# A decoder layer on one core: dense products whole or in four strips, score fills copied before their maxima

## The chip, the core and the metric

The kernel runs on one core of one Trainium2 chip, in one launch. The metric is the device time of that launch in microseconds, as the median of several runs. The engines are TensorE (PE in the profile, with PEld for its weight loads), VectorE (DVE), ScalarE (ACT), GpSimd (POOL) and SyncE (SP, which here only issues transfers). All data are fp32. One fp32 product appears in the trace as two passes, each a weight load (LDWEIGHTS) and a MATMUL.

## What is computed

There are 16 sequences of 512 tokens with 256 features, and for each a context of 64 rows. Each sequence goes through three blocks, each followed by a layernorm of input plus block:

```python
# 1. gated long convolution and MLP
z  = rmsnorm(u, pre_norm_w) @ in_proj_w.T          # 3 x 256 features
x2, x1, v = split(short_causal_conv3(z) + short_b)
xv = x1 * v
y  = (fftconv(xv, h) + xv * D_skip) * x2           # h: sum of 16 decaying exponentials per feature
y  = y @ out_proj_w.T + u
zm = rmsnorm(y, post_norm_w)
y  = y + (gelu(zm @ l1_w.T) * (zm @ l2_w.T)) @ l3_w.T      # 672 inner features
# 2. causal self attention plus attention to the context, 16 heads of 16
y  = softmax(causal(q k^T / 4)) v  +  softmax(qc kc^T / 4) vc
y  = y @ Wp + bp
# 3. low-rank feed-forward, rank 64, 1024 inner features
H  = gelu((x @ U1) @ V1 + b1);   y = (H @ U2) @ V2 + b2
```

## The kernel before

A front part computes the convolution for all sequences and loads the weights. The main part then works sequence by sequence (a "batch" below). The work is not written in the order in which it runs. Each piece is handed to `Plan.op` with the engines it may run on, an estimated cost, a priority (`prio`, lower is earlier), the buffers it reads and writes, and a function that emits the instructions. `Plan.schedule` plays this through engine by engine with the estimated costs, and `Plan.emit` writes the instructions in that order. So the order on each engine is fixed when the kernel is built, and a changed cost or rule can move work anywhere in it. Buffers come from small fixed sets: in PSUM one `scores` tile of four banks, one `av` bank and three `mm` banks; in SBUF among others three `ex` tiles of 128x2048.

TensorE can be used as one array of 128x128, or be divided: into four row groups of 32 (products of 32 rows, one per head), into column groups of 32 or 64, or both. The shape (rows, columns) of a part is the `tiling` of an op; `FULL` is 128x128. A stretch below is a run of matmuls with one tiling. `Plan.change` shifts priorities so that ops of one tiling gather: an op that would leave the whole array waits (`HOLD`, 1000), an op of the tiling in force goes first (`STAY`, 1000). Score fills are `urgent` and are held back by neither. `EMPTY` is the cost that the planner adds at a change of tiling.

The steps in the text, by their lines in the profile:

- Dense products on the whole array: the MLP's first two products L1187 and its third L1239, the output projection L1148, the value projection L1268, the query and key projections L1340 (`project`), the attention's output L1083 (`to_tokens`), the feed-forward's first and last L1761 and L1807, and the context's keys and values L1292 and L1317. The MLP's remaining 32 inner features are L1217, 128x32.
- Transposes L348, L1507 (of the maxima) and L1359, on the whole array; also L518 in the front.
- Score fills. Each takes the one `scores` tile, [128, 4 heads, 512]. Per batch there are 12 for the row maxima (L1435, 32x128; three per group of four heads, of 320+192, 448+64 and 512 columns), 10 for the exponentials (L1557, 32x128), and 2 against the context (L1615, 32x64).
- Maxima (`maxima`, `mx_op`): VectorE adds the causal mask to the diagonal blocks in PSUM (L1484) and takes maxima there (L1486, L1489, L1492, L1494, L1495, L1497). In the batches of `COPIED`, that is 0, 1, 13, 14 and 15, ScalarE instead copies the fill to an `ex` tile (L1458), GpSimd masks the copy with affine selects (L1465), and VectorE takes the maxima of the copy.
- Exponentials: ScalarE L1527 from the `scores` tile to an `ex` tile, GpSimd zeroes the upper triangle (L1574), and TensorE makes the weighted sums into `av` (L1587, 128x32; L1635 for the context, 64x32).
- Feed-forward: L1778 (64x128), gelu L1786 on ScalarE, L1794 (128x64).

In batches 0, 1 and 15 the fills are made and used in two halves. The MLP's and feed-forward's gelus and the attention's exponentials are kept in phases: a batch's gelus come between the exponentials of the batch before and its own. The feed-forward of batches 0 to 10 is planned beside the attention of batches 2 to 12, that of 11 and 12 beside batch 15, and that of 13 to 15 at the end; batches 13 and 14 have none beside them.

```python
COPIED = (0, 1, B - 3, B - 2, B - 1)
```

Of the kernel before, what the change touches and what calls it, by code (L numbers as in the profile page):

```python
# [24 lines left out]
FULL = (P, P)  # L25
SLOT_OF = (1, 0, 2, 3)
# [25 lines left out]
class Op:  # L52


    def __init__(self, n, engines, cost, lat, prio, fn):
        self.n, self.engines, self.cost, self.lat, self.prio, self.fn = n, engines, cost, lat, prio, fn
        self.deps, self.users, self.bufs = set(), [], []
        self.ready, self.start, self.end, self.engine = 0.0, None, None, None
        self.tiling, self.urgent = FULL, False


class Plan:
# [9 lines left out]
    def __init__(self, tiles, hold=0, stay=0):  # L72
        self.tiles, self.ops = tiles, []
        self.HOLD, self.STAY = hold, stay

    EMPTY = {P: 0.215, P // 2: 0.16, P // 4: 0.145}

    def op(self, engines, cost, fn, prio, r=(), w=(), lat=0.0, after=(), tiling=FULL, urgent=False, holds=()):
        o = Op(len(self.ops), engines.split(), cost, lat, prio, fn)
        o.tiling, o.urgent = tiling, urgent  # L80
# [14 lines left out]
    def change(self, o, tiling):  # L95

        if o.tiling == tiling:
            return -self.STAY if tiling != FULL else 0
        if o.urgent or o.tiling == FULL:
            return 0  # L100
        return self.HOLD if tiling == FULL else -self.STAY / 2

    def schedule(self):
# [29 lines left out]
        while left:  # L133
# [4 lines left out]
            for e in self.ENGINES:  # L138
# [24 lines left out]
                if e == "PE" and o.tiling != tiling:  # L163
                    o.empty = self.EMPTY[tiling[1]]
                    tiling = o.tiling
                else:
                    o.empty = 0.0
# [22 lines left out]
    def emit(self):  # L190
        for o in self.schedule():
            for b in o.bufs:
                b.t = self.tiles[b.cls][b.slot[1]]
            o.fn(o.engine)
# [3 lines left out]
def decoder_layer(  # L198
# [96 lines left out]
    ROWS4, ROWS2, COLS4, COLS2, BOTH = (SLOT, P), (P // 2, P), (P, SLOT), (P, P // 2), (P // 2, SLOT)  # L295
# [76 lines left out]
    with ExitStack() as front:  # L372
# [283 lines left out]
        for blk in range(NR // R8):  # L656
# [43 lines left out]
            plan.op("PE", 1.0, near_mm, pc - 60, r=[XV[kh], NEAR], w=[ps], tiling=COLS4, holds=[st])  # L700
# [61 lines left out]
            far_done = plan.op("PE", 1.0, far_mm, pc + 10, r=[st, far], w=ys, tiling=(SLOT, P // 2))  # L762
# [270 lines left out]
    plan = Plan(pool, 1000, 1000)  # L1033
# [40 lines left out]
    def to_tokens(xT, w, res, prio):  # L1074

        for cp in range(NT // 2):
            ps = Buf("mm")
            for cc in range(2):

                for k in range(KD):  # L1080

                    def mm(e, cp=cp, cc=cc, k=k, ps=ps):
                        nc.tensor.matmul(  # L1083
# [4 lines left out]
                    plan.op("PE", pe(D), mm, prio, r=[xT], w=[ps])  # L1088
# [18 lines left out]
    def first_block(b, after):  # L1107
# [33 lines left out]
        for cp in range(NT // 2):  # L1141
            ps = Buf("mm")
            for cc in range(2):

                for k in range(KD):

                    def outp(e, cp=cp, cc=cc, k=k, ps=ps):
                        nc.tensor.matmul(  # L1148
# [4 lines left out]
                    plan.op("PE", pe(D), outp, p0, r=[(yt, k)], w=[ps], after=after)  # L1153
# [26 lines left out]
        for f in range(NF):  # L1180
            halves = []
            for w in (w_l1, w_l2):
                ps = Buf("mm")
                for k in range(KD):

                    def mm(e, f=f, w=w, k=k, ps=ps):
                        nc.tensor.matmul(  # L1187
# [3 lines left out]
                    gelus_pe[b].append(plan.op("PE", pe(T), mm, p1 - k, r=[(zT, k)], w=[ps]))  # L1191
# [21 lines left out]
        def mm_e(e, ps=ps):  # L1213
            for n, w in enumerate((w_l1, w_l2)):
                for k in range(KD):
                    for c in range(NT):
                        nc.tensor.matmul(  # L1217
# [4 lines left out]
        gelus_pe[b].append(plan.op("PE", 0.88, mm_e, p1, r=[zT], w=[ps], tiling=COLS4))  # L1222
# [10 lines left out]
        for cp in range(NT // 2):  # L1233
            ps = Buf("mm")
            for cc in range(2):
                for f in range(NF + 1):

                    def mm(e, c=2 * cp + cc, cc=cc, f=f, ps=ps):
                        nc.tensor.matmul(  # L1239
# [6 lines left out]
                    plan.op("PE", pe(D), mm, p2, r=[(gT, f) if f < NF else gE], w=[ps])  # L1246
# [4 lines left out]
    def attention(b, x_):  # L1251
# [9 lines left out]
        for jp in range(NT // 2):  # L1261
            ps = Buf("mm")
            for jj in range(2):

                for k in range(KD):

                    def mm(e, jp=jp, jj=jj, k=k, ps=ps):
                        nc.tensor.matmul(  # L1268
# [4 lines left out]
                    plan.op("PE", pe(D), mm, p0 + 40, r=[(xT, k)], w=[ps])  # L1273
# [12 lines left out]
        if b % 2 == 0:  # L1286
# [3 lines left out]
            def kc_mm(e, ps=ps):  # L1290
                for g in range(G):
                    nc.tensor.matmul(  # L1292
# [4 lines left out]
            plan.op("PE", 0.9, kc_mm, p0, w=[ps], after=begun)  # L1297
# [19 lines left out]
            lambda e, ps=ps: nc.tensor.matmul(  # L1317
                ps.t[:, 0:D], twice.t.rearrange("c s t -> c (s t)"), wcv_s, start=True, stop=True
            ),
            p0 + 45, r=[twice], w=[ps],  # L1320
# [13 lines left out]
        def project(dst, w, cols, bias, prio):  # L1334
            ps = Buf("mm")

            for k in range(KD):

                def mm(e, k=k):
                    nc.tensor.matmul(ps.t, w[:, k, cols], xT.t[:, k, :], start=(k == 0), stop=(k == KD - 1))  # L1340

                plan.op("PE", pe(T), mm, prio - k, r=[(xT, k)], w=[ps], holds=[dst])
# [63 lines left out]
        def maxima(g):  # L1406
# [8 lines left out]
            for use in (((1, TC), (0, TC)), ((2, TC), (3, None)), ((3, 0),)):  # L1415
# [10 lines left out]
                for h, cols in enumerate(cuts):  # L1426

                    def mm(e, use=use, sc=sc, cols=cols):
                        at = 0
                        for i, first in use:  # L1430
                            k0, k1 = (0, TC) if first is None else (TC - first, TC + (i + 1) * P)
                            lo, hi = max(at, cols.start), min(at + k1 - k0, cols.stop)
                            for r in range(HPG if lo < hi else 0):
                                hd = bass.ts(r, SLOT)
                                nc.tensor.matmul(  # L1435
# [6 lines left out]
                        "PE", cost_pe / len(cuts), mm, ps_, r=[q, kk], w=[(sc, h)], tiling=ROWS4, urgent=True  # L1442
# [8 lines left out]
                if b in COPIED:  # L1451
# [18 lines left out]
                    n = HPG * P * (2 if use[0][0] == 1 else 1)  # L1470
                    plan.op("POOL", 0.65 * n / (HPG * P), masked, ps_ - 6, w=[both])
                    sc, cost = both, cost - dve(n)

                def mx_op(e, sc=sc, i=use[0][0], diagonal=diagonal):
                    own = mx.t[:, :, :, HD + par : HD + par + 1]
                    ctx_ = mx.t[:, :, :, par : par + 1].rearrange("p i r o -> p r i o")
                    by_64 = sc.t.rearrange("p r (a c) -> p r a c", c=TC)
                    if b not in COPIED:
                        diag, mask = diagonal(sc.t), mask_qk.unsqueeze(1)
                        if i == 1:  # L1480
                            mask = mask.unsqueeze(1).to_broadcast([P, HPG, 2, P])
                        else:
                            mask = mask.to_broadcast([P, HPG, P])
                        nc.vector.tensor_tensor(diag, diag, mask, ALU.add)  # L1484
                    if i == 1:
                        nc.vector.tensor_reduce(  # L1486
                            ctx_[:, :, SLOT_OF[1] : SLOT_OF[1] + 2, :], by_64[:, :, 0:6:5, :], AX.X, ALU.max, negate=True
                        )
                        nc.vector.tensor_reduce(  # L1489
# [441 lines left out]
```

## Time and profile before

| | |
|---|---|
| runs | 2082.22, 2083.39, 2087.12 us; median 2083.39 |
| span of the profiled execution | 2082.0 us, first to last instruction; the median run is 1.4 us above it |
| granted TensorE clock | 0.992 of full over the span |
| TensorE | 2005.5 us busy (96%), 14,900 passes and as many weight loads |
| VectorE, ScalarE, GpSimd | 1331.5 (64%), 1029.1 (49%), 768.5 us (37%) |
| instruction queue q8 | 117 packets, 1.92 MB (16 KB each) |
| transfers | 88 GB/s on average; 27.6% of the 16 engines' span |

Busy time of an engine is the union of its instructions' times; matmuls that run abreast are counted once. The ends of matmuls are modelled, so a PE that is called busy need not be streaming; the text reads distances from start to start. The trace gives no time of the profiled execution besides its span; the lowest run is 0.2 us above that span.

Group rows read: line, engine, operation, output<-inputs, shape of the weights (rows*columns of the array), shapes, count | busy us, mean ns of one. The mean of matmuls that run four abreast is the time of one of them, while busy us / count is its share.

### The profile page before, as it was taken

The numbers are of one execution on the slowest core, as the hardware profiler recorded it, in microseconds if no ns is written. First come the engines' busy times: TensorE is split into PE (matmuls) and PEld (weight loads), VectorE is DVE, ScalarE is ACT, GpSimd is POOL, SyncE is SP. The second block draws the span as 40 slices with busy tenths as digits, with TensorE's granted clock in tenths as the row PEclk, the third lists the DMA queues.
The fourth block names the chain that finished last, engine by engine and source line by source line (L and its number), as shares of the span: only waits on it lengthen the run. The fifth ranks groups of instructions, "written<-read, shape, count | busy, mean of one in ns | idle before, by whom it ended". The sixth has DMA issues, their size and how long they took to land. (4 is left out here: it accounts for less than half of the span.)

```text
span 2082.0 us, 36834 instructions
## 1 busy us (share of the span) xinstructions
PE 2005.5 (96%) x14900; PEld 1054.2 (51%) x14900; DVE 1331.5 (64%) x1922; ACT 1029.1 (49%) x1463; POOL 768.5 (37%) x1036
## 2 busy tenths in 40 slices
PE   8999978999999999999999999999999999999987
PEld 4455645555554545454545454454545454545443
DVE  7987543736584848484857576666767584656554
ACT  7863422656435262717161626253534446655773
POOL 7694622243323241414142424232323233533432
PEclk9999989999999999999999999999999999999999
DMA  5365861040304040313131312222131404031200
GB/s 200 109 211 179 269 221 51 6 119 17 119 11 144 12 134 22 123 33 118 37 108 48 100 56 88 68 71 85 58 98 33 123 13 129 17 101 44 72 22 31
DMA packets 114939, 182.22 MB, mean 88 GB/s; under 512 B 13393, under 2 KB 62034, under 8 KB 114642
## 3 DMA queue, kind: packets, MB, share of 16 engines
q1 hardware_dynamic: 113234, 177.26, 27.6%
q8 instruction: 117, 1.92, 0.4%
q10 hardware_dynamic: 1536, 2.62, 0.4%
q14 instruction: 52, 0.43, 0.1%
HBM read 111.09 MB, written 68.76 MB: 86 GB/s over the span
## 5 line engine op out<-in xcount | busy, mean ns | idle before, releaser
L1527 ACT ACTIVATE ex<-scores 128x2048 f32<-128x2048 f32 (+1 forms) x228 | 362.5, 1606 | 193.4 <-PE scores L1557 140.8
L1187 PE MATMUL mm<-xT,w_l 128*128 128x512 f32 x640 | 299.5, 608 | 0.0
L1574 POOL TENSOR_SCALAR_AFFINE_SELECT ex<-ex 128x512 f32<-128x512 f32 x256 | 159.1, 637 | 324.5 <-ACT ex L1527 323.1
L1435 PE MATMUL scores<-keys,q 32*128 32x192 f32 (+5 forms) x2848 | 225.3, 426 | 6.2 <-ACT ex L1458 4.6
L1557 PE MATMUL scores<-q,keys 32*128 32x256 f32 (+3 forms) x2240 | 183.3, 435 | 11.8 <-ACT ex L1527 10.9
L1435 PEld LDWEIGHTS scores<-keys,q 32*128 32x128 f32 x2848 | 123.8, 184 | 138.5 <-issue 41.1
L1786 ACT ACTIVATE row<-mm,b_s 128x512 f32<-128x512 f32 x124 | 79.0, 687 | 224.6 <-PE mm L1778 223.9
L1187 PEld LDWEIGHTS mm<-xT,w_l 128*128 128x128 f32 x640 | 114.5, 190 | 141.4 <-issue 133.9
L1717 POOL TENSOR_TENSOR nd<-nd,nd 128x1024 f32<-128x1024 f32 x30 | 70.8, 2358 | 299.2 <-DMA nd<-di 299.2
L1587 PE MATMUL av<-ex,va 128*32 128x512 f32 (+3 forms) x2048 | 164.8, 438 | 0.9 <-POOL ex L1574 0.9
L1239 PE MATMUL mm<-w_l,gT 128*128 128x256 f32 x640 | 160.6, 386 | 0.0
L308 POOL TENSOR_SCALAR small<-small 128x4 f32<-128x4 f32 (+1 forms) x66 | 13.3, 201 | 393.7 <-DVE small L1047 358.8
L500 DVE SCALAR_TENSOR_TENSOR frow<-fmm,cw,frow 128x511 f32<-128x511 f32 x192 | 141.1, 744 | 25.9 <-ACT frow L492 21.2
L1484 DVE TENSOR_TENSOR scores<-scores,mask_qk 128x1024 f32<-128x1024 f32 x132 | 115.6, 876 | 60.9 <-PE scores L1435 57.8
L1557 PEld LDWEIGHTS scores<-q,keys 32*128 32x128 f32 x2240 | 96.9, 184 | 107.5 <-ACT ex L1527 67.0
L1199 ACT ACTIVATE row<-mm 128x512 f32<-128x512 f32 x80 | 47.8, 598 | 209.4 <-PE mm L1187 209.4
L1458 ACT COPY ex<-scores 128x1024 f32<-128x1024 f32 (+1 forms) x96 | 114.4, 1228 | 65.6 <-PE scores L1435 52.9
L485 PE MATMUL fmm<-fx,inw 128*128 128x512 f32 x312 | 143.4, 604 | 0.0
L1239 PEld LDWEIGHTS mm<-w_l,gT 128*128 128x128 f32 x640 | 117.2, 190 | 44.6 <-issue 31.1
L299 DVE COPY row<-av 128x512 f32<-128x512 f32 x60 | 41.5, 692 | 134.9 <-PE av L1587 124.5
L1340 PE MATMUL mm<-xT,wqc_s 128*128 128x512 f32 x256 | 126.3, 611 | 0.0
L1346 DVE TENSOR_SCALAR q<-mm,bqc_s 128x512 f32<-128x512 f32 x62 | 46.5, 750 | 100.4 <-PE mm L1340 100.3
(212 smaller groups left out, 3489.3 us busy)
## 6 DMA issues: line engine op xcount, KB each, us to landing
dn<-row SPq DMA_DIRECT2D x120, 256.0 KB
keys<-dk SPq DMA_DIRECT2D x64, 256.0 KB
nd<-dn SPq DMA_DIRECT2D x30, 512.0 KB
nd<-di SPq DMA_DIRECT2D x30, 512.0 KB
fx<-hpad SPq DMA_DIRECT2D x28, 512.0 KB
early<-gates SPq DMA_DIRECT2D x16, 512.0 KB
early<-yconv SPq DMA_DIRECT2D x32, 256.0 KB
dk<-row SPq DMA_DIRECT2D x32, 256.0 KB
```

What stands on the lines that cost most here:

```text
L485: nc.tensor.matmul(ps.t, inw[:, k, bass.ts(m, P)], xT.t[:, k, :], start=(k == 0), stop=(k == KD - 1))
L500: lambda e, lag=lag: nc.vector.scalar_tensor_tensor(t.t[:, lag:], ps.t[:, 0 : T - lag], cw[:, m, 2 - lag : 3 - lag], t.t[:, lag:], ALU.mul ...
L1187: nc.tensor.matmul(ps.t, w[:, k, bass.ts(f, P)], zT.t[:, k, :], start=(k == 0), stop=(k == KD - 1))
L1239: nc.tensor.matmul(ps.t[:, bass.ts(cc, D)], gT.t[:, f, bass.ts(c, P)] if f < NF else gE.t, w_l3[:, f, :] if f < NF else w_l3e[:, c, :], st ...
L1340: nc.tensor.matmul(ps.t, w[:, k, cols], xT.t[:, k, :], start=(k == 0), stop=(k == KD - 1))
L1435: nc.tensor.matmul(sc.t[:, r, lo:hi], q.t[hd, bass.ts(i, P)], kk.t[hd, k0 - at + lo : k0 - at + hi], start=True, stop=True,)
L1458: lambda e, sc=sc, both=both, cols=cols: nc.scalar.copy(both.t[:, :, cols], sc.t[:, :, cols]),
L1484: nc.vector.tensor_tensor(diag, diag, mask, ALU.add)
L1527: lambda e: nc.scalar.activation(ex.t.rearrange("p (r n) -> p r n", r=HPG)[:, :, cols], sc.t[:, :, cols], AF.Exp, scale=scale),
L1557: nc.tensor.matmul(sc.t[:, r, lo:hi], keys[g].t[hd, TC + j * P : TC + (j + 1) * P], qas[g].t[hd, q0 + lo : q0 + hi], start=True, stop=True,)
L1574: lambda e, ex=ex, at=at: nc.gpsimd.affine_select(out=ex.t.rearrange("p (r n) -> p r n", r=HPG)[:, :, at : at + P], in_=ex.t.rearrange("p ...
L1587: nc.tensor.matmul(av[g].t[bass.ts(r, SLOT), j * P :], va.t[:, j, h * VS : h * VS + SLOT], ex.t[:, r * T + at : r * T + at + n], start=(j ...
```

## The change

Three things change.

First, dense ops are marked `flex`. In the main part such an op is emitted by `Plan.matmul`, either as one product on the whole array or as four products of 32 columns each (`STRIPS`, 128x32). `Plan.mode` picks the form: as it stands if the array is whole or in strips, and strips from any other tiling. The whole array and strips both count as plain in `Plan.change`. Transposes stay whole.

Second, other tilings are brought to few: all scores use `ROWS` = 32x64 (so a fill's 32x128 product becomes two), the feed-forward's second product and the context's sums use `BOTH` = 64x32, and the feed-forward's third product uses strips. The planner's cost of a change becomes a formula of the old and the new tiling.

Third, `COPIED` takes in all batches, and `mx_op` becomes one op per reduction. The mask add of VectorE (L1484) is gone.

The same three changes in the diff, cut to its core:

```diff
+STRIPS = (P, SLOT)
...
-    EMPTY = {P: 0.215, P // 2: 0.16, P // 4: 0.145}
+    ENTRY = {P: 0.104, P // 2: 0.051, P // 4: 0.024}
+
+    def empty(self, old, new):
+
+        return 0.0 if old == new else 0.087 + 0.0066 * P * P / (old[0] * old[1]) + self.ENTRY[new[1]]
...
     def change(self, o, tiling):
 
-        if o.tiling == tiling:
-            return -self.STAY if tiling != FULL else 0
+        want, plain = self.mode(o, tiling), (FULL, STRIPS) if self.strips else (FULL,)
+        if want == tiling:
+            return -self.STAY if tiling not in plain else 0
         if o.urgent or o.tiling == FULL:
             return 0
-        return self.HOLD if tiling == FULL else -self.STAY / 2
+        return self.HOLD if tiling in plain else -self.STAY / 2
+
+    def mode(self, o, tiling):
+
+        return (tiling if tiling in (FULL, STRIPS) else STRIPS) if o.flex else o.tiling
+
+    def matmul(self, out, weights, moving, **kw):
+
+        rows, cols = self.now
+        n = weights.shape[-1]
+        for c in range(0, n, cols):
+            cs = slice(c, min(c + cols, n))
+            self.nc.tensor.matmul(out[cs], weights[:, cs], moving, **kw)
...
-    ROWS4, ROWS2, COLS4, COLS2, BOTH = (SLOT, P), (P // 2, P), (P, SLOT), (P, P // 2), (P // 2, SLOT)
+    COLS2, ROWS, BOTH = (P, P // 2), (SLOT, P // 2), (P // 2, SLOT)
...
-                        nc.tensor.matmul(
+                        plan.matmul(
                             ps.t, w[:, k, bass.ts(f, P)], zT.t[:, k, :], start=(k == 0), stop=(k == KD - 1)
                         )
 
-                    gelus_pe[b].append(plan.op("PE", pe(T), mm, p1 - k, r=[(zT, k)], w=[ps]))
+                    gelus_pe[b].append(plan.op("PE", pe(T), mm, p1 - k, r=[(zT, k)], w=[ps], flex=True))
...
-                        "PE", cost_pe / len(cuts), mm, ps_, r=[q, kk], w=[(sc, h)], tiling=ROWS4, urgent=True
+                        "PE", cost_pe / len(cuts), mm, ps_, r=[q, kk], w=[(sc, h)], tiling=ROWS, urgent=True
...
-                plan.op("DVE", cost, mx_op, ps_ - 5, r=[sc], w=[(mx, par)])
+                for n, (size, views) in enumerate(reduces):
+
+                    def reduce(e, views=views):
+                        dst, src = views()
+                        nc.vector.tensor_reduce(dst, src, AX.X, ALU.max, negate=True)
+
+                    plan.op("DVE", dve(HPG * size), reduce, ps_ - 5, r=[sc], w=[(mx, (par, use[0][0], n))])
...
             def hm(e, fp=fp, bank=bank):
-                for s in range(2):
-                    half = bass.ts(s, RANK)
-                    nc.tensor.matmul(bank(s), v1_s[half, bass.ts(fp, P)], pT.t[half, :], start=True, stop=True)
+                for c in range(0, P, SLOT):
+                    for s in range(2):
+                        half, at = bass.ts(s, RANK), fp * P + c
+                        plan.matmul(bank(s)[c : c + SLOT], v1_s[half, at : at + SLOT], pT.t[half, :], start=True, stop=True)
...
-    COPIED = (0, 1, B - 3, B - 2, B - 1)
+    COPIED = range(B)
```

The other dense products get `plan.matmul` and `flex=True` in the same way, the other fills `ROWS`, and L1794's op `STRIPS`.

## The prediction

> **What bounds it now.** I read the page first, then busy time by batch, then who waits for whom, then the order of TensorE's work. The page names TensorE, and its slices show that this holds almost everywhere:
>
> ```profile
> PE 2005.5 (96%) x14900; PEld 1054.2 (51%) x14900; DVE 1331.5 (64%) x1922; ACT 1029.1 (49%) x1463; POOL 768.5 (37%) x1036
> PE   8999978999999999999999999999999999999987
> ```
>
> A batch begins where its first L1435 fill starts: 452.8 us for batch 1, 990.3 for 6, 1098.4 for 7, 1749.4 for 13, 1941.8 for 15; batches 2 to 12 take 108 to 109 us each. Busy time by such stretches (stretch, length, PE, PEld, DVE, ACT, POOL):
>
> ```profile
> 990.30:1098.40 108.10, 107.77 (x751) 54.45 (x750) 71.35 (x101) 47.91 (x62) 33.67 (x44) 1.00 0.24 75
> 1749.40:1847.10 97.70, 96.70 (x715) 50.78 (x714) 59.79 (x83) 60.67 (x57) 42.77 (x58) 1.00 0.19 57
> 1847.10:1941.80 94.70, 92.76 (x655) 45.08 (x654) 58.05 (x80) 55.59 (x42) 32.20 (x49) 1.00 0.22 68
> ```
>
> TensorE idles 0.33 us in batch 6. Batches 13 and 14 already copy and mask as the change does everywhere; there it idles 1.0 and 1.9. ScalarE's waits in batch 6 point at TensorE, not the other way:
>
> ```profile
> ACT row L1786 <- PE mm L1778: 18.3, 3, 14.7
> ACT row L1199 <- PE mm L1187: 17.3, 5, 4.2
> ACT ex L1527 <- PE scores L1557: 9.5, 8, 2.0
> ```
>
> But a busy TensorE is not one that streams. In its order of time (start, length, line, shape of the weights, count of passes; one fp32 product is two passes):
>
> ```profile
> 1001.89 3.70 PE L1187 MATMUL mm<-xT,w_l 128*128 128x512 f32 x8
> 1005.52 1.15 PE L1435 MATMUL scores<-keys,q 32*128 32x320 f32 x16
> 1006.60 4.56 PE L1187 MATMUL mm<-xT,w_l 128*128 128x512 f32 x10
> 1011.09 1.20 PE L1435 MATMUL scores<-keys,q 32*128 32x448 f32 x16
> 1012.22 2.84 PE L1187 MATMUL mm<-xT,w_l 128*128 128x512 f32 x6
> ...
> 1057.70 1.06 PE L1587 MATMUL av<-ex,va 128*32 128x512 f32 x8
> 1058.69 1.56 PE L1148 MATMUL mm<-outw,early 128*128 128x256 f32 x6
> ...
> 1071.16 1.11 PE L1615 MATMUL scores<-q,kcs 32*64 32x512 f32 x16
> 1072.20 1.13 PE L1340 MATMUL mm<-xT,wqc_s 128*128 128x512 f32 x2
> ...
> 1077.05 1.09 PE L1635 MATMUL mm<-ex,vc 64*32 64x512 f32 x16
> 1078.07 0.66 PE L348 MATMUL mm<-ident,y 128*128 128x128 f32 x4
> ```
>
> From start to start, 8 whole passes take 3.63 us and 10 take 4.49: 0.43 each (0.427 within a stretch), so a stretch costs 3.63 - 8 x 0.427 = 0.2 us besides its passes. The tiled stretches in view hold two rounds of 512 columns, 0.853 us, so L1587 (four abreast, 128x32) costs 0.99 - 0.853 = 0.14 extra, L1615 (eight, 32x64) 1.04 - 0.853 = 0.19, L1635 (eight, 64x32) 0.165. Medians over the trace: whole 0.198, 32x128 0.217, 64x128 0.204, 128x64 0.151, 128x32 0.137, 32x64 0.191, 64x32 0.164. These are the change of tiling and the first load of weights, exposed. The kernel has 1,083 stretches.
>
> **Part 1: tilings.** From 452.8 to 1941.8 us (batches 1 to 14) the trace holds 885 stretches: 328 whole, 309 of 32x128, 35 of 64x128, 44 of 128x64, 113 of 128x32, 28 each of 32x64 and 64x32. Times the prices: 64.9 + 67.1 + 7.1 + 6.6 + 15.5 + 5.3 + 4.6 = 171 us. I relabel the same order by the diff: L1435, L1557 and L1615 become 32x64; L1778 and L1635 64x32; L1794, L1587 and L1217 128x32; a flexible dense product takes 128x32, unless a transpose (L348, L1507) has just made the array whole. That leaves 806: 78 whole, 328 of 128x32, 337 of 32x64, 63 of 64x32, so 15.4 + 44.9 + 64.4 + 10.3 = 135 us. Saved: 36 us, on the path throughout, as TensorE idles 0.3 us a batch there. Outside, relabelling saves 2.3 us before and 2.7 after; those stretches have idle time (the tail is 118.34 busy of 140.20), so I count 2. The planner may put an order with fewer whole stretches in place of the old one: 0 to 10 us more, not counted.
>
> The passes themselves should cost the same. Strips of 128x32 run four abreast: 512 L1587 passes of 512 columns take 68.2 us busy, 133 ns each, 0.53 per four with their share of the changes; L1615 at eight abreast 29.0 us for 416, 0.56 per eight; a whole L1187 pass 299.5 / 640 = 0.47. A 24-pass L1587 stretch comes out 16 ns over its price, so the bound for strips is 0 to 1 ns a pass. No row has four strips reading the same moving columns; I take the same rate, because L1587's four already read four different ones.
>
> A page speaks against this: the Trainium skill, "TensorEngine Tiling (Array Packing)", section Instruction Overhead, gives each matmul about 60 cycles of overhead. Taken one after another at the 2.4 GHz of the skill's "TensorE: Matmul & The Clock Gate" (its opening table), 13,174 more passes would be an estimated 329 us, and the sum 2375 us. The trace disagrees: sixteen L1615 passes cost 0.19 us beyond streaming, all told.
>
> The 448+64 fills (L1435 at 1011.09) take 1.13 us against 1.07 for L1557's eight-pass fill: a weight load of 128 columns outlasts 64 columns of moving data. With 64-column loads most of that 0.06 goes; about 60 fills, 3 us.
>
> **Instructions.** Relabelled, 2,354 dense passes become four, 5,088 score passes two, L1778's and L1794's passes four and two: 14,900 grows to 28,074, each with its weight load. The instruction queue's 117 packets of 16 KB become about 219. After 480 us the mean rate rises from 14 to 29 instructions a us. Nothing waited for a packet there; in the front, at 60 a us, L745 waited up to 2.3 us for "issue" around a fetch. Bound 0 to 20 us; I take 1, since 256 instructions still last some 8 us.
>
> **Part 2: copies.** Batches 2 to 12 have 132 maxima fills. VectorE loses its mask adds: 61.4 + 54.2 = 115.6 us (L1484). ScalarE gains 132 copies of 1.867 us (L1458) = 246, to 1,275 or 62% of the new span; per batch 47.9 + 22.4 = 70 of some 105. GpSimd gains 176 selects of 0.637 (L1465) = 112. Both have idle time, and the reductions take the same from copies (2.28 against 2.29 us). The one scores tile is freed after 1.87 us instead of 1.23 + 0.69 + 1.22 + 0.68 = 3.8, 3.1 or 3.0: three fills hold it 5.6 us, not 9.9. Batch 6's twelve maxima fills, 990.3 to 1052.4 us, need at least 12 x 1.07 + 4 x 9.9 + 12 x 0.35 for the hand-overs = 56.6 of their 62.1; with copies about 39. So the chain fills-to-maxima, close behind TensorE, moves away, and TensorE is late next. New waits: the next fill waits for ScalarE, behind whose copy gelus and evacuations queue; the reductions wait for GpSimd, and behind its masks queue the gate and divide products (2.36 us each at most). A copying batch idled TensorE 0.7 to 1.6 us more than batch 6: 8 to 18 us over eleven, though batches 13 and 14 have no feed-forward products to fill in; at best the present 0.33 goes, -4. I take +4, nearer the low end because these batches keep that filler.
>
> **Sum.** 2082.0 - 36 - 2 - 3 + 1 + 4 = 2046; the median run stands 1.4 us over the span: **2047 us**, 1.7% less. What a measurement here can tell from no change is 0.3%, 6 us.
>
> **Rivals.**
> - *Better order* (0.07): besides, the planner drops whole stretches (10) and the waits inside the paired L1778 stretches shrink (9 of 3.01 us, where passes and price make 1.91: about 10 us in all). 2047 - 20 = 2027, and 2019 with the copies at -4.
> - *ScalarE holds the scores tile* (0.13): its copies come late behind gelus and exponentials, as 70 us of 105 in order leave less slack. Price: the 18 us bound and up to twice it in place of 4, 2061 to 2079. For: "scores <- ACT" waits already exist. Against: ScalarE at 62% in batch 13 cost TensorE 1 us. It cancels the gain at 0.3 us per copied fill.
> - *Instruction supply* (0.12, mostly the slower side): strips double the instructions, fetches come 2 to 3 us late in the middle already (359 instructions between two, where a packet holds 256), and a packet missed costs 2.3 us as at L745. Slower by 6 us needs 42 / 2.3 = 18 stalls among some 180 fetches after 450 us, one in ten; one in five gives 2130. Against: before, none in the middle, and the front ran 600 instructions in 10 us without one.
> - *Forecast* (0.68): 2030 to 2061, by the copies at -4 to 18 and half of the better order.
>
> **Numbers.** Faster: 0.68 + 0.07 + 0.10 of ScalarE's 0.13 = 0.85; the same: 0.03 + 0.02 of supply's = 0.05; slower: 0.10. The range 2029 to 2078 leaves out about 0.05 below and 0.14 above.
>
> **What would show it.** Right: some 28,000 PE passes, about 990 stretches, 128x32 the commonest shape on L1187, L1239 and L1340; batches 2 to 12 at 105 to 106 us; L1484's group gone, L1458 with 132 more; PE still at 99% there. ScalarE rival: "PE scores <- ACT ex" of tens of us. Supply rival: PE waits on "issue" of 1 to 3 us beside instruction packets. The forecast is wrong if a stretch of dense strips takes longer from start to start than 0.427 us a pass, by even 15 ns: 2,354 x 15 ns = 35 us.

## The result and the profile after

The kernel after takes 2112.56 us (median of 4 runs, 2109.03 to 2119.49) against 2083.86 us for the kernel before on the same chip: a ratio of 1.014 [1.0118, 1.0163]. It is slower by 1.4%; the prediction was 2047 us, with a range of 2029 to 2078. The profiled execution took 2110.6 us, its span is 2108.9 us, 26.9 us longer than before.

Two lines of the page of the kernel after, busy time and the slices:

```profile
PE 1978.7 (94%) x27210; PEld 887.1 (42%) x27210; DVE 1237.1 (59%) x1828; ACT 1248.9 (59%) x1557; POOL 877.9 (42%) x1212
PE   8999888899987999999999999999999999989787
```

The passes nearly doubled, and TensorE is busy 26.8 us less than before. But it now idles 2108.9 - 1978.7 = 130.2 us, against 76.5 before. The idle time isn't spread: the slices show 8 in places that had 9, and 7 near the end. By stretches of the kernel after (stretch, length, PE, PEld, DVE, ACT, POOL, then the granted clock, the DMA share and GB/s):

```profile
553.10:635.00 81.90, 76.20 (x923) 34.94 (x923) 54.15 (x75) 40.47 (x50) 28.05 (x35) 1.00 0.18 56
635.00:785.60 150.60, 138.57 (x2073) 55.73 (x2072) 74.09 (x114) 95.93 (x91) 56.21 (x85) 0.99 0.27 83
1001.50:1107.20 105.70, 104.40 (x1477) 42.46 (x1473) 63.94 (x93) 65.48 (x67) 43.03 (x60) 1.00 0.25 72
1953.00:2106.00 153.00, 124.02 (x2016) 50.69 (x2012) 81.14 (x154) 89.90 (x120) 46.76 (x74) 0.95 0.10 31
```

A middle batch (1001.5) is as forecast, 105.7 us, though its neighbours take 110.2. Batches 2 and 3 (the first two rows) and the tail (the last, which ends 2.9 us before the span does) hold 17.7 and 29 us of idle time. Batch by batch, from first maxima fill to first maxima fill, in the profiled executions; two experiments stand beside them:

| us | before | after | e1: old order | e12: one constant |
|---|---|---|---|---|
| up to batch 2 | 554.9 | 553.1 | 555.8 | 554.2 |
| batches 2 and 3 | 218.5 | 232.5 | 212.6 | 217.0 |
| batches 4 to 12 | 976.0 | 969.7 | 951.3 | 960.3 |
| batch 13 | 97.7 | 96.9 | 95.1 | 96.6 |
| batch 14 | 94.7 | 100.8 | 91.8 | 92.8 |
| batch 15 and tail | 140.2 | 155.9 | 139.8 | 138.2 |
| span | 2082.0 | 2108.9 | 2046.4 | 2059.1 |

So three places lose 14.0, 6.1 and 15.7 us, and the middle gains 6.3 where it should have gained some 25 (e1 gains 24.7). In that middle TensorE idles 20.1 us of 969.7, against 3.9 of 951.4 in e1; so most of the difference is waiting.

What a stretch costs is as predicted. TensorE in its order of time, kernel after (L122 is the line of `plan.matmul`, which now records all products but transposes):

```profile
1003.56 1.92 PE L122 MATMUL mm<-xT,w_l 128*32 128x512 f32 x16
1005.42 1.12 PE L122 MATMUL scores<-keys,q 32*64 32x448 f32 x32
1006.47 2.78 PE L122 MATMUL mm<-xT,w_l 128*32 128x512 f32 x24
1009.18 1.11 PE L122 MATMUL scores<-keys,q 32*64 32x512 f32 x16
```

A 448+64 fill takes 1006.47 - 1005.42 = 1.05 us (1.13 before), and 24 strips 2.71 (six rounds of 0.427 and 0.14 for the change: 2.70). The trace holds 976 stretches where about 990 were forecast.

What is new is what TensorE waits for (the waits of PE over the span, kernel after: engine, line, releaser, us in total, times, longest):

```profile
PE scores L122 <- ACT ex L1480: 26.6, 31, 2.1
PE scores L122 <- ACT ex L1553: 24.2, 30, 2.1
```

That is 50.8 us of fills that wait for ScalarE's copies (L1480) and exponentials (L1553); before, the like rows added up to 15.5. ScalarE itself in the batch at 1001.5 still waits for TensorE (its waits in that batch):

```profile
ACT ex L1480 <- PE scores L122: 12.1, 11, 1.9
ACT ex L1553 <- PE scores L122: 7.7, 8, 2.0
```

Both waits are true at once: the fill waits for the one `scores` tile to be read, and ScalarE for the fill. A chain of fill, read, fill runs at its own pace of over 3 us, and TensorE is only idle in it where it has nothing else to do. Why it has nothing else is to be seen in its order around 615 us, kernel after (`row,v_s` is the feed-forward's second product, `scores<-q,keys` a fill for exponentials):

```profile
613.94 1.09 PE L122 MATMUL mm<-row,v_s 64*32 64x512 f32 x16
614.96 1.06 PE L122 MATMUL av<-row,u_s 128*32 128x512 f32 x8
...
618.72 3.64 PE L122 MATMUL mm<-outw,early 128*32 128x256 f32 x64
...
635.00 1.12 PE L122 MATMUL scores<-keys,q 32*64 32x320 f32 x32
636.05 1.09 PE L122 MATMUL mm<-row,v_s 64*32 64x512 f32 x16
638.14 1.12 PE L122 MATMUL scores<-q,keys 32*64 32x512 f32 x16 [1.01 <-ACT ex L1480]
...
642.50 2.01 PE L122 MATMUL scores<-q,keys 32*64 32x384 f32 x32 [2.14 <-ACT ex L1553]
```

The last of the four second products comes at 636.05, 22 us after the third. The exponentials' fills depend on all four (the phases: a batch's gelus before its exponentials), so the first of them is at 638.14. From 616.98 to 635.00 TensorE works off the next batch's projections and output products in plain tilings, with no fill among them; then the exponentials run without those products, and up to 785.6 their fills wait 10.9 us for ScalarE's exponentials. The same stretch in e12, the kernel after with one constant of the planner changed:

```profile
612.54 1.09 PE L122 MATMUL mm<-row,v_s 64*32 64x512 f32 x16
613.56 1.07 PE L122 MATMUL av<-row,u_s 128*32 128x512 f32 x8
614.56 1.09 PE L122 MATMUL mm<-row,v_s 64*32 64x512 f32 x16
...
616.58 1.11 PE L122 MATMUL scores<-q,keys 32*64 32x512 f32 x16
...
626.66 1.48 PE L122 MATMUL mm<-outw,early 128*32 128x256 f32 x24
```

Here the fourth product is in place at 614.56, the exponentials begin at 616.58, and the projections and output products lie between their fills.

The code says how a product can be held. `hm` (L1778 before) is not urgent, so in a plain tiling `Plan.change` puts it back by 1000, the distance in priority between two batches, and it goes only when nothing that then ranks before it is ready, the next batch's dense products among it. Before, the third product that precedes it (128x64) was no plain tiling, and from there `change` drew it forward by 500. Now the third product, the weighted sums and the dense products are all in strips, and strips count as plain.

### The profile page after: what moved, and what is told of

The parts are those of the page before. It is cut to its first block, busy times and chain, and to the rows that moved or that the text cites. A ratio compares the mean times of both kernels' runs of the same rounds, so it can differ in the third digit from the quotient of the medians.

```text
span 2108.9 us, 61825 instructions
## 1 busy us (share of the span) xinstructions
PE 1978.7 (94%) x27210; PEld 887.1 (42%) x27210; DVE 1237.1 (59%) x1828; ACT 1248.9 (59%) x1557; POOL 877.9 (42%) x1212
## 4 chain that ended last, share of the span: by engine, by line
PE 59%; ACT 8%; DVE 4%; issue 2%; DMA 2%; POOL 1%; SPq 0%; POOLq 0%; ACTq 0%; DVEq 0%
PE mm L122 36%; PE scores L122 15%; PE av L122 7%; ACT ex L1553 3%; DVE maxes L1523 2%; ACT ex L1480 2%; PE mm L370 1%; ACT row L1813 1%; DVE q L1542 1%; ACT xt L1089 1%; PE mm L1533 1%; ACT L1553 1%; DMA nd<-di 1%; DMA di<-sums 1%; POOL nd L1743 1%
## 5 line engine op out<-in xcount | busy, mean ns | idle before, releaser
L1523 DVE TENSOR_REDUCE maxes<-ex 128x8 f32<-128x512 f32 (+4 forms) x384 | 448.3, 1210 | 69.4 <-POOL ex L1487 60.0
L1480 ACT COPY ex<-scores 128x2048 f32<-128x2048 f32 (+1 forms) x228 | 360.6, 1598 | 209.5 <-PE scores L122 181.2
L1553 ACT ACTIVATE ex<-scores 128x2048 f32<-128x2048 f32 (+1 forms) x228 | 362.4, 1606 | 163.5 <-PE scores L122 148.6
L122 PE MATMUL mm<-xT,w_l 128*32 128x512 f32 (+2 forms) x2880 | 318.2, 541 | 4.1 <-DVE gT L1226 4.0
L1487 POOL TENSOR_SCALAR_AFFINE_SELECT ex<-ex 128x512 f32<-128x512 f32 x256 | 159.5, 638 | 385.5 <-ACT ex L1480 385.4
L1600 POOL TENSOR_SCALAR_AFFINE_SELECT ex<-ex 128x512 f32<-128x512 f32 x256 | 159.3, 637 | 305.9 <-ACT ex L1553 305.2
L122 PE MATMUL scores<-keys,q 32*64 32x192 f32 (+5 forms) x5696 | 219.9, 410 | 23.7 <-ACT ex L1480 23.6
L122 PE MATMUL scores<-q,keys 32*64 32x256 f32 (+3 forms) x4480 | 181.7, 423 | 25.3 <-ACT ex L1553 20.9
L122 PEld LDWEIGHTS scores<-keys,q 32*64 32x64 f32 x5696 | 103.4, 132 | 176.2 <-ACT ex L1480 100.2
L122 PE MATMUL av<-ex,va 128*32 128x512 f32 (+3 forms) x2048 | 167.4, 438 | 2.4 <-POOL ex L1600 2.3
L122 PE MATMUL mm<-w_l,gT 128*32 128x256 f32 (+1 forms) x1900 | 164.2, 387 | 2.4 <-DVE q L1542 2.4
L122 PEld LDWEIGHTS mm<-xT,w_l 128*32 128x32 f32 (+1 forms) x2880 | 88.2, 111 | 175.3 <-issue 154.4
L122 PEld LDWEIGHTS scores<-q,keys 32*64 32x64 f32 x4480 | 80.2, 131 | 141.8 <-ACT ex L1553 79.0
L122 PE MATMUL mm<-xT,wqc_s 128*32 128x512 f32 (+1 forms) x802 | 123.8, 594 | 0.0
L122 PEld LDWEIGHTS mm<-w_l,gT 128*32 128x32 f32 (+1 forms) x1900 | 91.4, 120 | 71.7 <-issue 38.7
```

The source lines that it names most:

```text
L122: self.nc.tensor.matmul(out[cs], weights[:, cs], moving, **kw)
L1480: lambda e, sc=sc, both=both, cols=cols: nc.scalar.copy(both.t[:, :, cols], sc.t[:, :, cols]),
L1487: nc.gpsimd.affine_select(out=part, in_=part, compare_op=ALU.is_ge, fill=NEG, base=0, pattern=[[0, HPG], [-1, P]], channel_multiplier=1,)
L1523: nc.vector.tensor_reduce(dst, src, AX.X, ALU.max, negate=True)
L1553: lambda e: nc.scalar.activation(ex.t.rearrange("p (r n) -> p r n", r=HPG)[:, :, cols], sc.t[:, :, cols], AF.Exp, scale=scale),
L1600: lambda e, ex=ex, at=at: nc.gpsimd.affine_select(out=ex.t.rearrange("p (r n) -> p r n", r=HPG)[:, :, at : at + P], in_=ex.t.rearrange("p ...
```

## The experiments

Times are medians of 3 rounds, ratios against the kernel before on the same chip. The runs stand on several chips, on which the kernel before takes 2082.6 to 2084.4 us; so a difference between two runs of different chips is good to some 2 us.

**The order or the prices.** e1 emits all new tilings, but plans the order with the old tilings, the old `EMPTY` table and the old rule; copies in the five batches and maxima in one op, as before:

```diff
-    tiling=ROWS, urgent=True
+    tiling=ROWS4, made=ROWS, urgent=True      # planned as, emitted as; so for every op
-    COPIED = range(B)
+    COPIED = (0, 1, B - 3, B - 2, B - 1)
```

> The order on every engine is that of the kernel before (planned with its tilings, its costs and its rule), and maxima are taken as before; only the tilings that are emitted are those of the change. The trace of after shows the price of each stretch as predicted. Theory A (the loss comes with the order that the planner makes): about 2083.9 - 36 - 2 - 3 = 2043 us, 1.9% under before, about 990 stretches. Rival C (the strips themselves do harm, by their instructions or on the engines around them): no gain, 2080 to 2115.

2044.72 us, 0.9813 [0.9799, 0.9828], the fastest kernel of this study. This is the prediction's sum without its copies, 2082 - 36 - 2 - 3 + 1 + 1.4 = 2043. From batch 1 to batch 14 the trace of e1 holds the 806 stretches of the relabelling, shape by shape (78, 328, 337 and 63), and these batches take 1451.9 us against 1489.0. A middle batch (980.10 on, kernel e1; PE busy 104.86 of 105.30):

```profile
980.10:1085.40 105.30, 104.86 (x1553) 42.53 (x1549) 71.01 (x101) 48.01 (x62) 33.61 (x44) 1.00 0.25 76
```

e2 is the change with its own rule and formula, only `COPIED` and `mx_op` as before:

> The tilings, the planner's costs and its rule of the change; copies in batches 0, 1, 13, 14 and 15 alone, as before. If the loss of after (some 70 us of waits, against 45 saved on stretches) comes with the copies: about 2045 us. If it comes with the order under the new rule: 2090 to 2115.

2194.44 us, 1.0532 [1.0516, 1.0548], outside both expected ranges. Without the copies the loss is nearly four times as large, so it doesn't need the copies. In its middle batches a second product is left behind each time: one is at 1085.73, the last at 1108.31, and between them lie 17 us of plain products.

e3 adds the copies alone to the kernel before (`COPIED = range(B)`), e4 also splits `mx_op` into one op per reduction:

> The kernel before with copies in all batches, the maxima of a fill still one op. If the loss comes with the copies: 2083.9 + 50 to 70 = 2135 to 2155 us, with TensorE waiting for ScalarE ahead of fills. If it comes with the new rule: within 10 us of before.

> As the run with copies alone, but with one op for each reduction, as in the change. If the size of the op matters (a shorter op lets other VectorE work in between): 5 us or more under that run; otherwise the same as it within 5 us.

2092.89 us, 1.0046 [1.0028, 1.0063], and 2097.15 us, 1.0065 [1.0049, 1.0082]. Copies cost a little at the old tilings (8.5 us). Splitting the maxima adds 4.3 us by the medians, which isn't clear of the noise: the intervals overlap, and from batch 2 on the two profiles have the same times batch by batch to 0.1 us.

**The second product.** e5 is the kernel after, e6 is e2, each with one word:

```diff
-    plan.op("PE", tiled(T), hm, p3, r=[pT], w=hp, tiling=BOTH)
+    plan.op("PE", tiled(T), hm, p3, r=[pT], w=hp, tiling=BOTH, urgent=True)
```

> The changed kernel, with one word more: the feed-forward's second product (64x32, line L1778 of the kernel before) is marked urgent, so the planner no longer adds 1000 to its rank while the array is whole or in strips. Theory H: this product is held until a fill opens another tiling; the exponentials' fills may only come after its gelus; so both stand still while the next batch's dense products run, and the exponentials later lack filler. Then most of the 68 us between after and the old order come back: 2050 to 2070 us. Rival (the copies, or the rest of the new rule): 2095 us or more.

> The tilings with the new rule, copies in five batches alone, and the feed-forward's second product urgent. Theory H: from 2194 to 2050 to 2080 us, with TensorE's waits for ScalarE ahead of exponentials' fills down from 122 us to under 40. Rival (another part of the new rule): over 2150 us.

e6: 2066.33 us, 0.9931 [0.991, 0.9952], 128 us less than e2. The wait of e2 that goes (PE waits of e2, then of e6, by the same line):

```profile
PE scores L122 <- ACT ex L1549: 122.2, 123, 2.4
```

```profile
PE scores L122 <- ACT ex L1549: 19.8, 24, 1.7
```

So e2's loss was the held product. The other profiles agree: only in the kernel after, e2, e13 and e18 does batch 2's fourth second product come 20 us or more after the third (in all others within 6 us). Batches 2 and 3 of the kernel after, e13 and e18 take 231.2 to 232.9 us, and e2, where a product is held in every middle batch, takes 1065.9 for batches 4 to 12; the others take 211.8 to 222.0 and 949.6 to 987.5. e5 took 2094.71 us, 1.0059 [1.0039, 1.008]: 18 us less than the kernel after, but where the rival put it and not at 2050 to 2070. The loss in batches 2 and 3 is gone (217.8 against 232.5), but batches 4 to 12 now take 985.1 against 969.7.

**The steps one by one.** e7 is e1 with the copies everywhere; e8 is e7 planned with the formula, in place of the table, for the tilings as emitted:

> All three parts of the change are emitted, but the order is planned with the tilings, costs and rule of the kernel before (copies in all batches, one op per fill). Copies alone cost 2092.9 - 2084.4 = 8.5 us and the tilings in the old order gain 39.7: if they add up, 2053 us; if copies pay once TensorE has less to do, 2044 or less.

> As the run before it in this list, but with the change's formula for the cost of a change of tiling, worked out for the tilings that are emitted. If the rule alone did the harm, within 10 us of that run; if the formula did part of it, 20 us or more above.

2058.55 us, 0.9889 [0.987, 0.9908], and 2089.44 us, 1.0035 [1.0025, 1.0045]. This makes a ladder: tilings 2083.9 to 2044.7 (-39.7 on its chip), copies +13.8, formula +30.9, new rule with `mx_op` split +23.1 to 2112.6. The prediction had nothing for the formula, since on average its prices are those of the trace: a middle batch of e1 has 58 stretches (24 of 32x64, 23 of 128x32, 6 whole, 5 of 64x32), by the prediction's medians 9.7 us or 0.17 each, and the formula charges 9.6 for the 57 changes between them. The table charges 0.145 to 0.215 us for a change.

**Slack or chance?** A table that charges too much leaves the plan slack: TensorE runs late in the plan, and work that waits for another engine finds it ready. e9 to e12 give the formula 0.04 us more per change (e10 instead takes the copies out of e8):

```diff
-        return 0.0 if old == new else 0.087 + ...
+        return 0.0 if old == new else 0.127 + ...
```

> The new tilings, copies in every batch, the old rule and the change's formula for the cost of a change of tiling (2089.4 us), with 0.04 us added to the formula's constant (0.087 to 0.127), so that the plan is charged about 0.21 us a change, as with the old table, where the measured price is 0.17. Theory S (the plan needs the slack: with the measured price TensorE runs ahead of the other engines in the plan and the order leaves them no time): 2055 to 2070, the tail's rest back near 20 us. Theory N (it is the difference of prices between tilings, or plain luck of the order): 2078 to 2100, the tail's rest still near 40.

> The new tilings in an order planned with the old rule and the change's formula, copies only in the five batches that had them (with the old table this order took 2044.7 us). If the formula costs its 31 us by itself: 2068 to 2085. If it costs only where ScalarE has the copies to make as well: 2042 to 2055.

> All of the change but the copies, the feed-forward's second product marked urgent (2066.3 us), with 0.04 us added to the formula's constant. That kernel rests 1 to 2 us in a middle batch, but 12.8 in batch 14 and 36.4 in the tail, against 2.9 and 19.9 in the old order. Theory S: batch 14 and the tail come back, 2040 to 2058. Theory N: 2060 to 2075.

> The kernel after (2112.6 us) with 0.04 us added to the formula's constant and nothing else. If the formula's lack of slack and the new rule each cost their part (31 and 23 us): 2078 to 2090, with the rest of 24 us in batches 2 and 3 still there. If the slack alone is enough: 2055 to 2070. If the slack does nothing: 2100 to 2125.

e9 2067.77 us, 0.9924 [0.991, 0.9939]: 22 less than e8. e10 2070.16 us, 0.9933 [0.9917, 0.995]: the formula costs 25 us without copies too. e11 2075.17 us, 0.9961 [0.9946, 0.9976]: 9 us more than e6 (6 by the ratios), against slack. e12, the kernel after with this one constant, 2063.72 us, 0.9906 [0.9891, 0.9921]: 49 us less. Two for slack and one against, so the next four went further both ways: the kernel after at 0.107 and 0.187, and e2 at 0.067 and 0.137.

> The kernel after with the formula's constant at 0.107 (0.087 took 2112.6 us, 0.127 took 2063.7). Theory S (slack: a little more of it, a little fewer waits): between them, 2075 to 2100. Theory L (each constant is another order, and the order falls well or badly): anywhere from 2055 to 2125, with whole-batch differences in place of a shift of every batch.

> The kernel after with the formula's constant at 0.187, a charge of about 0.27 us a change, 0.1 over the measured price. Theory S: enough slack stays enough, 2055 to 2070. Theory L: 2070 to 2125, as the order falls.

> All of the change but the copies (2194.4 us) with the formula's constant lowered from 0.087 to 0.067 and no product marked urgent. Theory S: less slack, so no better: 2185 or more. Theory L: another order, in which the feed-forward's last second product may come before TensorE stays in plain tilings: below 2130.

> All of the change but the copies (2194.4 us) with the formula's constant raised from 0.087 to 0.137 and no product marked urgent. Theory S: better, 2050 to 2150. Theory L: another order, 2050 to 2200. If the plain-tilings rule alone made the loss of 128 us, whatever the charges: 2170 or more.

| constant | 0.067 | 0.087 (the change) | 0.107 | 0.127 | 0.137 | 0.187 |
|---|---|---|---|---|---|---|
| with all copies (after) | | 2112.6 | 2100.9 | 2063.7 | | 2106.6 |
| copies in five batches (e2) | 2095.9 | 2194.4 | | | 2057.0 | |

The ratios of e13 to e16 are 1.0074 [1.0054, 1.0094], 1.0103 [1.0079, 1.0126], 1.0054 [1.0038, 1.0071] and 0.9863 [0.9845, 0.9882]. e13 (1 us over its range) and e16 fit slack; but e14 loses 43 us against e12 with more slack, and e15 gains 99 us against e2 with less. Slack falls as the cause, and the time isn't a smooth function of the charge. The rule isn't a cost of its own either: at 0.127 the new rule with the split (e12, 2063.7) is 4 us faster than the old (e9, 2067.8).

**The tail.** In all 18 profiles up to here the stretch from batch 15's first fill on takes 138 to 143 us (before, e1, e3, e4, e7, e9, e12, e16) or 149 to 161 (the others). In every long one the last second product that the exponentials need comes after batch 15's last maxima fill, and the first exponentials' fill starts 1.5 us (once 2.9) after that product's last pass; in every short one the product comes before. Kernel after, then e12:

```profile
1992.04 1.12 PE L122 MATMUL scores<-keys,q 32*64 32x256 f32 x32
...
2008.74 1.09 PE L122 MATMUL mm<-row,v_s 64*32 64x512 f32 x16
...
2010.76 1.12 PE L122 MATMUL scores<-q,keys 32*64 32x256 f32 x32
```

```profile
1948.84 1.09 PE L122 MATMUL mm<-row,v_s 64*32 64x512 f32 x16
...
1959.87 1.12 PE L122 MATMUL scores<-keys,q 32*64 32x256 f32 x32 [0.72 <-ACT ex L1480]
...
1963.08 1.12 PE L122 MATMUL scores<-q,keys 32*64 32x256 f32 x32 [1.08 <-ACT ex L1480]
```

From the last maxima fill to the first exponentials' fill it is 18.7 us in the one and 3.2 in the other; the tails differ by 17.7. In the kernel after the last second products come behind three waits of TensorE for VectorE (1.9 to 3.2 us each, between 1993 and 2002). e17 (on e6) and e18 (on the kernel after) change the place of that product, by planning batch 11's feed-forward one batch earlier:

```diff
-    B if b >= 11 else b + 3)
+    B if b >= 12 else B - 1 if b == 11 else b + 3)
```

> All of the change but the copies, the second product urgent (2066.3 us), and the feed-forward of batch 11 planned beside batch 14's attention in place of batch 15's. That leaves four second products, not eight, to be done before batch 15's exponentials may start, and gives batch 14 some 10 us of products to fill in. If the long tail (154.8 us against 139.8 in the old order) comes from exponentials that wait for the last second product: batch 14 and the tail, 255 us together, come to 225 to 240, and the time to 2038 to 2052. If the tail is long for another reason: only moved work, 2060 to 2072.

> The kernel after (2112.6 us), nothing changed but the same move of batch 11's feed-forward. If the tail and batch 14 lose to the late second products: 257 us together come to 230 to 245, the loss in batches 2 and 3 stays, 2084 to 2100. If the tail is long for another reason: 2105 to 2120.

e17: 2054.04 us, 0.9862 [0.984, 0.9885], 12 us less than e6. Batch 14 and the tail take 100.4 + 137.8 = 238.2 us against 255.2, within the expected span; the time missed its range by 2 us. The last second product lies before the last maxima fill, and from that fill to the first exponentials' fill it is 3.2 us (19.8 in e6):

```profile
1961.97 1.12 PE L122 MATMUL scores<-keys,q 32*64 32x256 f32 x32 [1.15 <-ACT ex L1480]
1965.17 1.12 PE L122 MATMUL scores<-q,keys 32*64 32x256 f32 x32 [2.08 <-ACT ex L1480]
```

That is 16.6 us of the 16.9 by which the tail is shorter. But the move also takes products out of the tail, where TensorE is busy 108.7 us against 121.1, and into idle time of batch 14; the two effects aren't separated.

e18: 2117.02 us, 1.0158 [1.0141, 1.0175], a miss. Its tail's product is early as well, but the four moved ones are now held in batch 14 as in batch 2: batch 14's exponentials start 84.7 us after its first fill, 0.5 us behind the last pass of the last second product (in batch 2 of the kernel after: 85.0). Batch 14 and the tail together take 258.7 us, as before 256.7. The loss moved with the products, one batch ahead.

## Why the prediction was wrong

The prices stood. e1 is within 2 us of the sum for the tilings, and batches 1 to 14 take 37.1 us less, where 36 for the stretches and most of the 3 for the 448+64 fills were forecast. So the stretch prices and the strips' rate hold; the 1 us for instructions is too small to be told apart. The page against the change, "TensorEngine Tiling (Array Packing)" of the Trainium skill, section Instruction Overhead, doesn't hold here if its 60 cycles are taken one after another, as in the prediction's estimate of 329 us: e1 has 28,074 - 14,900 = 13,174 more passes and took 39.7 us less.

**The step that failed** is the last sentence of part 1: "The planner may put an order with fewer whole stretches in place of the old one: 0 to 10 us more, not counted". I priced the old order under new labels and took the new order for a bonus that can't hurt. The formula and the rule were read in the diff as bookkeeping, and got no term; on the ladder they cost 30.9 and, with the split, 23.1 us. With the same tilings and copies in every batch, eight kernels that differ only in the planner's rule, numbers and marks and in the split (e5, e7, e8, e9, e12, e13, e14 and the kernel after) span 2058.6 to 2112.6 us, and without the added copies seven (e1, e2, e6, e10, e11, e15, e16) span 2044.7 to 2194.4. The range of 49 us held no part of that. The slowdown of 1.4% is one draw from such orders and not what the new shapes or the copies cost. What could be read ahead: `hm` was not urgent, its predecessor's tiling became plain, and the exponentials depend on it.

**The copies** were sized at +4, with -4 to 18 as bounds. They cost 13.8 (e1 to e7) and 8.5 at the old tilings (e3): in the bounds, mis-sized by some 10. By the profiles of e1 and e7 only a part is waiting: TensorE idles 3.1 us more and is busy 7.2 us more, in 1,024 stretches against 993. So the copies too brought a new order, with 31 more stretches, which at 0.17 us each are an estimated 5 us; the prediction looked for their cost in waits alone.

**ScalarE holds the scores tile** named the row that would show it, "PE scores <- ACT ex" of tens of us, and it came: 50.8. But the mechanism is another. e12 has the same copies, 28.0 us in those rows and 49 us less time, and e2, without the added copies, has 122.2 + 8.7 = 130.9 us in its like rows. The waits are what is left when the filler has been used up. **Instruction supply** did not decide: 213 packets of 16 KB, and TensorE's waits on "issue" add up to 8.6 us, all on lines of the front, as the 8.6 before. **Better order** did not come: no new order of this study beats the old one, neither without the added copies (e1) nor with them (e7).

What stays open: for the middle batches of e5, e14 and e15 (109.0 to 109.7 us on average) I have found no one cause. That the late product makes the loss is shown for e2 by e6, and for batches 2 and 3 of the kernel after by e5 and by the profiles side by side. For the tail it rests on the 18 profiles and on e17, which also moved work out of the tail. Why each constant places the product where it does was not followed through the planner.

## What to carry to other kernels

When a schedule is made by a planner, its costs and rules are part of the kernel: price a change of them as a new order, with a range on both sides as wide as such orders have been seen to differ, here over 50 us. Test a change of instruction shapes in the old order first; of the runs here only e1 showed what the shapes are worth. In a plan with phases, look for the op that ends a phase and ask which rule can now hold it: one product that came 22 us late emptied the next phase of its filler.

## What the runs showed of the hardware

Waits of about 2 us can halve TensorE's clock. In batch 14 of the kernel after four fills follow one another with nothing between. Its order of time, then a window before and the window of the slow fills, with the granted clock as the third number from the end:

```profile
1885.22 1.12 PE L122 MATMUL scores<-keys,q 32*64 32x320 f32 x32 [1.02 <-ACT ex L1480]
1888.41 2.02 PE L122 MATMUL scores<-keys,q 32*64 32x448 f32 x32 [2.06 <-ACT ex L1480]
1892.44 2.02 PE L122 MATMUL scores<-keys,q 32*64 32x512 f32 x16 [2.02 <-ACT ex L1480]
```

```profile
1886.00:1888.00 2.00, 0.34 (x19) 0.00 (x0) 2.00 (x2) 1.51 (x1) 0.00 (x0) 1.00 0.03 8
1888.41:1901.99 13.58, 9.54 (x96) 2.94 (x96) 9.18 (x10) 6.89 (x4) 2.63 (x5) 0.50 0.00 0
```

After 2.06 us of waiting the clock is 0.50, and a fill of as many columns takes 2.02 us in place of 1.12. The wait itself stays at 2.02 us, since it is for ScalarE's copy of 1.87 us; so a round of fill and copy takes 4.03 us (1888.41 to 1892.44) in place of 3.19 (1885.22 to 1888.41). The clock was back at 1901.93, after 5.5 us of unbroken work from 1896.48 on; in another place, at 645.83, after 3.3 us from 642.50 on. Not every such wait does it: a wait of 2.39 us from 593.4 on left the clock at 1.00, as did e2's waits of 1.0 to 1.4 us. In the kernel after the clock stands from 400 us on at 0.50 in four places before the end of the span, for 3.41, 13.65, 10.24 and 3.41 us: one, four, three and one times the same length. In the 3.41 us before the drop at 1888.28 TensorE was busy for 1.12. The mean clock of 0.984 against 0.992 means 2 x 0.016 x 2108.9 - 2 x 0.008 x 2082.0 = 34 us more at half rate, an estimated 17 us of streaming at most. So a wait of 2 us can cost more than 2 us: part of the loss in batch 14 and the tail is this.

The Trainium skill, "TensorE: Matmul & The Clock Gate", Part 1, puts the halving after an idle window of about 3.4 us and the return after as much busy time. The return after 3.3 us agrees; the halving came here after some 2 us of idling, and not each time.
